# Layer norm in a graph network kernel: group statistics assembled on GpSimd, shifts made on GpSimd

## The chip, the cores and the metric

The kernel runs on one core of one Trainium2 chip. The metric is device time in microseconds, the median over runs. A core has five engines with an instruction queue each, worked off in order: TensorE (PE, matrix products; PEld is its weight loads), VectorE (DVE), ScalarE (ACT), GpSimd (POOL, which also issues the indirect DMAs that gather rows by a list of indices) and SyncE (SP, which issues most other DMAs). An instruction that waits on a semaphore holds up everything behind it in its own queue.

## The reference

A graph of 6250 nodes with 256 channels and 100000 edges. The input is layer-normed over its channels and passed through a ReLU; four rounds of "add the neighbours' rows, three dense layers" follow, and the input is added at the end.

```python
def _layernorm(x, axis=-1, eps=1e-05):
    m = jnp.mean(x, axis=axis, keepdims=True)
    v = jnp.var(x, axis=axis, keepdims=True)
    return (x - m) / jnp.sqrt(v + eps)

h = jnp.maximum(_layernorm(x, axis=-1), 0.0)
x = x + _L0_gnn_ref(h, src, dst, ...)
# in it, for each of 4 layers: h = x + agg(x); three dense layers, ReLU between
```

## The kernel before

The 6250 nodes are 49 blocks of 128 rows, one row to a partition. The kernel first prepares (to about 130 us), then runs the four layers as long chains of matrix products over a count matrix that it builds from the edge lists, with part of the neighbours' rows gathered by GpSimd. Only the preparation is touched by the change; no later instruction moves in any queue.

The preparation interleaves several pieces of work, each written as a generator that gives up control after a short step. The order in which the steps are called is written out by hand, under a manual schedule, so each engine's queue holds its instructions in exactly that order. The pieces that matter here:

- `normed` (the norm). Blocks are loaded in groups of six: group 1 is blocks 0 to 5, group 9 is the last block alone. For a block, VectorE takes statistics of its 256 channels (`bn_stats`, L1007: six numbers, count, mean and a sum of squared distances for the even and for the odd channels) and puts the two halves together (`bn_aggr`, L1008: mean and variance into `mv`). When a group is through, ScalarE takes the square root of its variances (L1015, `std`), and VectorE makes `rstd` by a reciprocal (L1021) and `shift`, minus mean times rstd (L1022). These steps run ahead: the statistics of a pair of blocks are taken six pairs before that pair is scaled.
- For a pair of blocks, ScalarE then scales with ReLU (`h`, L1029), TensorE transposes (L1038), ScalarE copies the result out (`ht`, L1041), TensorE multiplies by the first weight (L1050, into `bp`), VectorE copies that out (`zs`, L1057), ScalarE rounds it (`XY`, high part, L1062), and GpSimd subtracts to get what the rounding left (`XY`, low part, L1067; for four pairs in the middle VectorE does it). SP stores `zs` to a table.
- `look` reads the sorted edge list. VectorE and ScalarE count edges against limits (L768, L771), which gives `starts` (L779). GpSimd then issues 16 indirect gathers (`wd`, L687), four at once and then two between steps of the norm. Four times VectorE unpacks a quarter of them (`hi`, L802, `rel`, L804, `hi`, L806), ScalarE casts (`f`, L807), TensorE transposes (L813) and ScalarE writes the result (`clT`, `cN`, L816, L818).
- `ranking` works on `cN` of all four quarters (L904, L910, L915 to L981). The end of the preparation waits for it and for the last block of the norm.
- `fused` multiplies weight matrices, with a small copy of a bias on GpSimd (L655) for each of three products.

Of the kernel before, what the change touches and what calls it, by code (L numbers as in the profile page):

```python
# [9 lines left out]
F32 = mybir.dt.float32  # L10
# [5 lines left out]
AF = mybir.ActivationFunctionType  # L16
OP = mybir.AluOpType
PSUM = bass.MemoryType.PSUM
DRAM = bass.MemoryType.DRAM
P = 128  # L20
# [400 lines left out]
def sorted_edges(  # L421
# [39 lines left out]
    nc = tc.nc  # L461
    N, C = x.shape
# [84 lines left out]
    eps = const.tile([P, 1], F32, name="eps")  # L547
# [8 lines left out]
    def rows_io(ap, t0, n, sb, load):  # L556

        whole = n if t0 + n < NT or LAST == P else n - 1
        got = []
        if whole:  # L560
            d = ap[t0 * P:(t0 + whole) * P, :].rearrange("(t p) c -> p t c", p=P)
            s = sb[:, :whole, :]
            got.append(nc.sync.dma_start(out=s if load else d, in_=d if load else s))
        if whole < n:
            for r0, r1 in ((0, LAST // 16 * 16), (LAST // 16 * 16, LAST)):
                d = ap[(t0 + whole) * P + r0:(t0 + whole) * P + r1, :]
                s = sb[r0:r1, whole, :]
                got.append(nc.sync.dma_start(out=s if load else d, in_=d if load else s))
        return got
# [31 lines left out]
    def load_w(name, ap, pool, queue, **kw):  # L601
        k = ap.shape[0] // P
        w = pool.tile([P, k, ap.shape[1]], F32, name=name, **kw)
        queue.dma_start(out=w, in_=ap.rearrange("(k p) n -> p k n", p=P))
        return w
# [66 lines left out]
    def after(ins, reason, what=None):  # L672

        what = paced if what is None else what
        if what:
            tc.add_manual_dep(
                ins.ins, what[0],
                mybir.DependencyInfo(mybir.DependencyClass.Sync,
                                     mybir.DependencyReason.DATA),
                reason=reason,  # L680
            )
# [303 lines left out]
    def normed(pool, ps_t, ps_z):  # L985
        G = 6
        w1 = load_w("w1_0", W1s[0], pool, nc.scalar, bufs=1)
        mv = pool.tile([P, NT, nc.vector.BN_AGGR_DIM], F32, name="mv", bufs=1)
        rstd = pool.tile([P, NT], F32, name="rstd", bufs=1)
        shift = pool.tile([P, NT], F32, name="shift", bufs=1)  # L990
        xs, h, ht, zp, zs, stds = {}, {}, {}, {}, {}, []
        pairs = [(i, min(2, NT - i)) for i in range(0, NT, 2)]

        def load(t0):
            n = min(G, NT - t0)
            xs[t0] = pool.tile([P, G, C], F32, name="xs", bufs=4)
            if t0 + n == NT and LAST < P:
                nc.gpsimd.memset(xs[t0][:, n - 1, :], 0.0)
            for got in rows_io(x, t0, n, xs[t0], True):
                if t0 == 2 * G:  # L1000
                    after(got, "the near edges come first", landed)

        def moments(s):
            i0, n = pairs[s]
            for i in range(i0, i0 + n):
                stats = pool.tile([P, nc.vector.BN_STATS_DIM], F32, name="stats", bufs=4)
                nc.vector.bn_stats(stats, xs[i // G * G][:, i % G, :])  # L1007
                got = nc.vector.bn_aggr(mv[:, i, :], stats)  # L1008
            if s == 2:
                landed[:] = [got.ins.name]  # L1010
            if (i0 + n) % G == 0 or i0 + n == NT:
                t0 = (i0 + n - 1) // G * G
                std = pool.tile([P, G], F32, name="std", bufs=2)
                m = i0 + n - t0
                nc.scalar.activation(std[:, :m], mv[:, t0:t0 + m, 1], AF.Sqrt, bias=eps)  # L1015
                stds.append((s, t0, m, std))

        def settle(s):
            while stds and stds[0][0] <= s:
                _, t0, m, std = stds.pop(0)  # L1020
                nc.vector.reciprocal(rstd[:, t0:t0 + m], std[:, :m])  # L1021
                nc.vector.scalar_tensor_tensor(shift[:, t0:t0 + m], mv[:, t0:t0 + m, 0], -1.0,  # L1022
                                               rstd[:, t0:t0 + m], op0=OP.mult, op1=OP.mult)

        def scale(s):
            i0, n = pairs[s]
            h[s] = pool.tile([P, 2, C], F32, name="h", bufs=2)
            for i in range(i0, i0 + n):
                nc.scalar.activation(h[s][:, i - i0, :], xs[i // G * G][:, i % G, :], AF.Relu,  # L1029
                                     bias=shift[:, i:i + 1], scale=rstd[:, i:i + 1])  # L1030

        def turn(s):
            n = pairs[s][1]
            hs = h.pop(s)
            pt = ps_t.tile([P, W], F32, name="agg")
            for c in range(KC):
                for i in range(n):
                    nc.tensor.transpose(pt[:, (c * 2 + i) * P:(c * 2 + i + 1) * P],  # L1038
                                        hs[:, i, c * P:(c + 1) * P], ident)
            ht[s] = pool.tile([P, KC, 2 * P], F32, name="ht", bufs=2)  # L1040
            nc.scalar.copy(ht[s][:, :, :n * P],  # L1041
                           pt.rearrange("p (c n) -> p c n", c=KC)[:, :, :n * P])

        def times(s):
            n = pairs[s][1]
            t = ht.pop(s)
            zp[s] = ps_z.tile([P, W], F32, name="bp")
            for i in range(n):
                for c in range(KC):
                    mm = nc.tensor.matmul(zp[s][:, i * C:(i + 1) * C], t[:, c, i * P:(i + 1) * P],  # L1050
                                          w1[:, c, :], start=(c == 0), stop=(c == KC - 1))
            paced[:] = [mm.ins.name]

        def out(s):
            n = pairs[s][1]
            zs[s] = pool.tile([P, 2, C], F32, name="zs", bufs=5)
            nc.vector.tensor_copy(zs[s][:, :n, :],  # L1057
                                  zp.pop(s)[:, :n * C].rearrange("p (i c) -> p i c", c=C))

        def high(s):  # L1060
            i0, n = pairs[s]
            nc.scalar.copy(XY[:, i0:i0 + n, :C], zs[s][:, :n, :])  # L1062

        def low(s):
            i0, n = pairs[s]
            engine = nc.vector if EASY[0] <= s < EASY[1] else nc.gpsimd
            engine.tensor_tensor(XY[:, i0:i0 + n, C:], zs[s][:, :n, :],  # L1067
                                    XY[:, i0:i0 + n, :C].bitcast(F32), OP.subtract)

        def keep(s):  # L1070
            i0, n = pairs[s]
            rows_io(tables[0], i0, n, zs.pop(s), False)

        for t0 in range(0, 2 * G, G):
            load(t0)
        yield
        for s in range(G):
            moments(s)
        settle(G)
        yield  # L1080
        for t0 in range(2 * G, 4 * G, G):
            load(t0)
        yield
        for s in range(len(pairs) + 5):
            if s % (G // 2) == 0 and s and s * 2 + 3 * G < NT:
                load(s * 2 + 3 * G)
            for lag, f in ((3, out), (4, high), (0, scale), (1, turn), (2, times), (-G, moments),
                           (4, low), (5, keep)):
                if 0 <= s - lag < len(pairs) and (f is not moments or s - lag >= G):
                    f(s - lag)  # L1090
                if f is turn:
                    yield
            settle(s + G - 1)
            yield
# [6 lines left out]
    with tc.manual_schedule():  # L1101
        with tc.tile_pool(name="prep", bufs=2) as prep, tc.tile_pool(
            name="ps_t", bufs=2, space=PSUM
# [3 lines left out]
            ranked = ranking(prep)  # L1107
            next(looked)
            rows = normed(prep, ps_t, ps_z)
            next(rows)  # L1110
            make_identity(nc, ident)
# [866 lines left out]
        with tc.tile_pool(name="hots", bufs=1) as hots, tc.tile_pool(  # L1978
            name="ats", bufs=1
        ) as ats, tc.tile_pool(name="rings", bufs=AHEAD + 2) as rings, tc.tile_pool(  # L1980
            name="gath", bufs=9
        ) as gath, tc.tile_pool(name="nd", bufs=1) as nd, tc.tile_pool(
            name="ps_a", bufs=2, space=PSUM
# [96 lines left out]
```

## Time and profile before

| what | value |
|---|---|
| median of 3 runs | 2004.05 us (2003.39 to 2004.16) |
| profiled execution, its own time | 1999.98 us |
| its span, first to last instruction | 1998.2 us, granted TensorE clock 0.976 on average |
| busy: PE, DVE, ACT, POOL | 1883.4, 1030.9, 1075.0, 1309.6 us |
| the preparation | the first 130 us or so |

Times in the profile count from the start of the span. "Idle before" names what ended an engine's wait. A view by stretches of time gives each engine's busy time in a stretch and the granted TensorE clock as a share of full speed; the timeline lists an engine's instructions with start and length; the chain of waits follows the work that ended last back to what released it at each step.

### The profile page before, as it was taken

The numbers are of one execution on the slowest core, as the hardware profiler recorded it, in microseconds if no ns is written. First come the engines' busy times: TensorE is split into PE (matmuls) and PEld (weight loads), VectorE is DVE, ScalarE is ACT, GpSimd is POOL, SyncE is SP. The second block draws the span as 40 slices with busy tenths as digits, with TensorE's granted clock in tenths as the row PEclk, the third lists the DMA queues.
The fourth block names the chain that finished last, engine by engine and source line by source line (L and its number), as shares of the span: only waits on it lengthen the run. The fifth ranks groups of instructions, "written<-read, shape, count | busy, mean of one in ns | idle before, by whom it ended". The sixth has DMA issues, their size and how long they took to land.

```text
span 1998.2 us, 29053 instructions
## 1 busy us (share of the span) xinstructions
PE 1883.4 (94%) x9236; PEld 1471.0 (74%) x9236; DVE 1030.9 (52%) x2211; ACT 1075.0 (54%) x2166; POOL 1309.6 (66%) x1447
## 2 busy tenths in 40 slices
PE   5856999999999899999999999999999999999997
PEld 3744777777777777777789777777788777777765
DVE  7887887676756343333335443433345354343433
ACT  4745776676767564444445464444445564454442
POOL 2526766766666556777777476676777366777775
PEclk9876999999999999999999999999999999999998
DMA  5524656666656575565557575564657476665653
GB/s 167 177 75 141 202 182 191 199 199 200 208 171 215 160 233 162 173 183 168 181 179 210 160 247 175 154 194 146 196 165 236 147 217 200 186 197 175 181 175 109
DMA packets 252334, 361.40 MB, mean 181 GB/s; under 512 B 33353, under 2 KB 206313, under 8 KB 252155
## 3 DMA queue, kind: packets, MB, share of 16 engines
q1 hardware_dynamic: 188160, 190.34, 30.2%
q0 software_dynamic: 61952, 166.87, 28.0%
q10 hardware_dynamic: 2058, 2.25, 0.4%
q8 instruction: 74, 1.21, 0.2%
q14 instruction: 90, 0.73, 0.1%
HBM read 292.33 MB, written 67.40 MB: 180 GB/s over the span
## 4 chain that ended last, share of the span: by engine, by line
PE 82%; DVE 7%; DMA 5%; issue 3%; POOL 2%; ACT 1%; SPq 0%; DVEq 0%; ACTq 0%; POOLq 0%
PE agg L1942 64%; PE ps L1519 6%; PE ps L1422 6%; DMA rows<-table,idxN 3%; PE bp L1259 2%; PE bp L1050 1%; DVE ws L768 1%; DVE hi L1205 1%; POOL rows L1627 1%; PE pt L1690 1%; POOL lane L1748 1%; DVE lo L1205 1%; PE ps L1436 1%; PE ps L1482 0%; ACT a L1913 0%
## 5 line engine op out<-in xcount | busy, mean ns | idle before, releaser
L1942 PE MATMUL agg<-a,XY 128*128 128x512 f32 (+1 forms) x6272 | 1508.8, 392 | 16.0 <-DVE a L1915 7.3
L1627 POOL DMA_INDIRECT rows<-table,idxN x1121 | 1084.5, 967 | 474.6 <-PE agg L1942 202.6
L1942 PEld LDWEIGHTS agg<-a,XY 128*128 128x128 f32 x6272 | 1142.6, 189 | 249.5 <-issue 12.4
L1913 ACT CAST a<-at 128x512 fp32r<-128x512 uint8 (+1 forms) x1249 | 707.3, 601 | 235.0 <-PE agg L1942 225.7
L1663 DVE TENSOR_TENSOR sums<-sums,rows 128x512 f32<-128x512 f32 x477 | 331.7, 695 | 502.2 <-DMA rows<-table,idxN 461.3
L1915 DVE CAST a<-at 128x512 fp32r<-128x512 uint8 (+1 forms) x312 | 142.0, 460 | 166.3 <-PE agg L1942 143.3
L1267 ACT CAST at<-bp 128x392 uint16<-128x392 f32 x227 | 110.0, 488 | 127.2 <-PE bp L1259 122.0
L1422 PE MATMUL ps<-h,w 128*128 128x512 f32 (+2 forms) x336 | 135.0, 545 | 0.3 <-DVE zz L1524 0.3
L1519 PE MATMUL ps<-w,h 128*128 128x256 f32 x588 | 133.9, 379 | 0.0
L1205 DVE TENSOR_TENSOR lo<-lanes,pairs 128x512 bf16<-128x512 bf16 x256 | 106.7, 422 | 45.6 <-PE bp L1259 44.9
L1259 PEld LDWEIGHTS <-lo 128*128 128x128 bf16 x1028 | 57.0, 102 | 97.3 <-DVE lo L1205 41.4
L1259 PE MATMUL bp<-hi,lo 128*128 128x98 bf16 x1028 | 94.4, 218 | 34.5 <-DVE lo L1205 27.7
L1519 PEld LDWEIGHTS ps<-w,h 128*128 128x128 f32 x588 | 111.5, 190 | 16.0
L596 POOL DMA_INDIRECT table<-zz,ids x72 | 72.5, 1007 | 68.3 <-DVE zz L1524 49.3
L1659 ACT COPY sums<-rows 128x512 f32<-128x512 f32 x74 | 43.8, 592 | 126.4 <-DMA rows<-table,idxN 91.2
L1425 ACT ACTIVATE h<-ps,bias 128x512 f32<-128x512 f32 (+2 forms) x84 | 51.6, 636 | 96.2 <-PE ps L1422 96.1
L1422 PEld LDWEIGHTS ps<-h,w 128*128 128x128 f32 x336 | 62.9, 192 | 52.8 <-issue 37.6
L1698 ACT ACTIVATE h<-pt,bias 128x256 f32<-128x256 f32 (+1 forms) x84 | 33.0, 444 | 127.7 <-PE pt L1690 127.7
L1524 DVE TENSOR_TENSOR zz<-ps,w 128x512 f32<-128x512 f32 (+1 forms) x81 | 50.5, 638 | 96.6 <-PE ps L1519 83.2
L1349 DVE TENSOR_TENSOR XY<-back,XY 128x256 fp32r<-128x256 f32 x138 | 54.7, 422 | 46.3 <-ACT XY L1348 45.9
L1956 ACT ACTIVATE h<-agg,bias 128x512 f32<-128x512 f32 (+1 forms) x60 | 37.3, 669 | 72.5 <-PE agg L1942 72.3
L1205 DVE TENSOR_TENSOR hi<-hi,pairs 128x784 bf16<-128x784 bf16 x128 | 72.7, 568 | 4.4
(239 smaller groups left out, 957.3 us busy)
## 6 DMA issues: line engine op xcount, KB each, us to landing
at<-mat SPq DMA_DIRECT2D x140, 448.0 KB
mat<-at SPq DMA_DIRECT2D x32, 784.0 KB
at<-mat SPq DMA_DIRECT2D x62, 336.0 KB
rows<-table,idxN POOLq DMA_INDIRECT x1121
back<-table SPq DMA_DIRECT2D x138, 128.0 KB
table<-zz SPq DMA_DIRECT2D x35, 256.0 KB
at<-mat SPq DMA_DIRECT2D x63, 112.0 KB
own<-zz SPq DMA_DIRECT2D x55, 128.0 KB
```

Of the source, the lines that this page charges most:

```text
L596: got = nc.gpsimd.indirect_dma_start(out=ap, out_offset=bass.IndirectOffsetOnAxis(ap=ids[:, b:b + 1], axis=0), in_=sb, in_offset=None)
L1205: nc.vector.tensor_tensor(o, values, which[:, :, None, :].to_broadcast(shape), op)
L1259: mm = nc.tensor.matmul(bp[:, m * HW:(m + 1) * HW], lo[:, m, :], hi[:, m, :], start=(i == 0), stop=(i == len(sets) - 1))
L1267: nc.scalar.copy(o, v)
L1349: later(1, lambda: nc.vector.tensor_tensor(XY[:, j:j + m, C:], z[:, :m, :], XY[:, j:j + m, :C].bitcast(F32), OP.subtract))
L1422: mm = nc.tensor.matmul(ps[:, :w], weights[l][0][:, c, i * P:(i + 1) * P], h1[:, c, :w], start=(c == 0), stop=(c == KC - 1))
L1519: mm = nc.tensor.matmul(o, h2[0][:, c, nodes], w3[:, c, :], start=(c == 0), stop=(c == KC - 1))
L1627: got = nc.gpsimd.indirect_dma_start(out=t[:, c % 2, :], out_offset=None, in_=tables[self.l][:, :], in_offset=bass.IndirectOffsetOnAxis(ap ...
L1663: nc.vector.tensor_tensor(sums, sums, rows.rearrange("p h c -> p (h c)"), OP.add)
L1913: nc.scalar.copy(o, v)
L1915: nc.vector.tensor_copy(o, v)
L1942: mm = nc.tensor.matmul(agg[c][:, :w], XY[:, j, o:o + P], a[:, :w], start=(i == 0 and half == 0), stop=(i == NT - 1 and half == 1))
```

## The change

From group 3 on, `bn_aggr` is gone. The six raw statistics of each block stay in one tile for the whole group, and when the group is through, GpSimd puts mean and variance together for up to six blocks at once in seven small instructions of 128 x 6: difference of the two means, sum of the means, sum of the squared distances, the difference scaled, squared, added to the sum, and the mean scaled by -0.5 (so `mv` then holds minus the mean). The square root on ScalarE carries the division by 256 in its scale. The shift becomes one product on GpSimd instead of VectorE. Groups 1 and 2 stay as they were.

```diff
         def moments(s):
             i0, n = pairs[s]
+            plain = i0 < 2 * G
             for i in range(i0, i0 + n):
-                stats = pool.tile([P, nc.vector.BN_STATS_DIM], F32, name="stats", bufs=4)
-                nc.vector.bn_stats(stats, xs[i // G * G][:, i % G, :])
-                got = nc.vector.bn_aggr(mv[:, i, :], stats)
+                if i % G == 0:
+                    parts[0] = pool.tile([P, G, nc.vector.BN_STATS_DIM], F32, name="stats", bufs=2)
+                stats = parts[0]
+                got = nc.vector.bn_stats(stats[:, i % G, :], xs[i // G * G][:, i % G, :])
+                if plain:
+                    got = nc.vector.bn_aggr(mv[:, i, :], stats[:, i % G, :])
...
-                nc.scalar.activation(std[:, :m], mv[:, t0:t0 + m, 1], AF.Sqrt, bias=eps)
+                mean, var = mv[:, t0:t0 + m, 0], mv[:, t0:t0 + m, 1]
+                if not plain:
+                    even, odd = (stats[:, :m, 3 * k:3 * k + 3] for k in range(2))
+                    apart = pool.tile([P, G], F32, name="apart", bufs=2)[:, :m]
+                    nc.gpsimd.tensor_tensor(apart, even[:, :, 1], odd[:, :, 1], OP.subtract)
+                    nc.gpsimd.tensor_tensor(mean, even[:, :, 1], odd[:, :, 1], OP.add)
+                    nc.gpsimd.tensor_tensor(var, even[:, :, 2], odd[:, :, 2], OP.add)
+                    nc.gpsimd.tensor_scalar(apart, apart, math.sqrt(C) / 2, None, op0=OP.mult)
+                    nc.gpsimd.tensor_tensor(apart, apart, apart, OP.mult)
+                    nc.gpsimd.tensor_tensor(var, var, apart, OP.add)
+                    nc.gpsimd.tensor_scalar(mean, mean, -0.5, None, op0=OP.mult)
+                nc.scalar.activation(std[:, :m], var, AF.Sqrt, bias=eps,
+                                     scale=1.0 if plain else 1.0 / C)
...
                 nc.vector.reciprocal(rstd[:, t0:t0 + m], std[:, :m])
-                nc.vector.scalar_tensor_tensor(shift[:, t0:t0 + m], mv[:, t0:t0 + m, 0], -1.0,
-                                               rstd[:, t0:t0 + m], op0=OP.mult, op1=OP.mult)
+                if t0 < 2 * G:
+                    nc.vector.scalar_tensor_tensor(shift[:, t0:t0 + m], mv[:, t0:t0 + m, 0], -1.0,
+                                                   rstd[:, t0:t0 + m], op0=OP.mult, op1=OP.mult)
+                else:
+                    nc.gpsimd.tensor_tensor(shift[:, t0:t0 + m], mv[:, t0:t0 + m, 0],
+                                            rstd[:, t0:t0 + m], OP.mult)
```

Where the instructions stand is seen in the queues. First GpSimd's, in the stretch of the gathers (L687), around the end of group 5; the low parts are L1067 before and L1087 after, since the code behind the edit moved by 20 lines. Before:

```order
L1067 TENSOR_TENSOR XY<-zs,XY 128x2x256
L687 DMA wd<-joined,starts 98x128 x2
L1067 TENSOR_TENSOR XY<-zs,XY 128x2x256
L687 DMA wd<-joined,starts 98x128 x2
L1067 TENSOR_TENSOR XY<-zs,XY 128x2x256
```

And now:

```order
L687 DMA wd<-joined,starts 98x128 x2
L1023 TENSOR_TENSOR apart<-stats 128x6
L1024 TENSOR_TENSOR mv<-stats 128x6
L1025 TENSOR_TENSOR mv<-stats 128x6
L1026 TENSOR_SCALAR apart<-apart 128x6
L1027 TENSOR_TENSOR apart<-apart 128x6
L1028 TENSOR_TENSOR mv<-mv,apart 128x6
L1029 TENSOR_SCALAR mv<-mv 128x6
L1087 TENSOR_TENSOR XY<-zs,XY 128x2x256
L687 DMA wd<-joined,starts 98x128 x2
L1087 TENSOR_TENSOR XY<-zs,XY 128x2x256
L1042 TENSOR_TENSOR shift<-mv,rstd 128x6
```

The seven stand behind gathers 7 and 8 and ahead of the low part and gathers 9 and 10; the shift of the group stands ahead of gathers 11 and 12. The seven of group 6 stand between gathers 14 and 15 in the same way, the shift of group 4 between gathers 4 and 5.

Second, ScalarE's queue at the same place, with what each instruction waits for (a semaphore of the named engine). Before:

```order
L1041 COPY ht<-agg 128x512 [waits PE_49,Activation_49]
L1015 ACTIVATE std<-mv,eps 128x6 [waits DVE_49]
L807 CAST f<-hi 98x512 [waits DVE_49]
L1062 CAST XY<-zs 128x2x256
L1029 ACTIVATE h<-xs,shift,rstd 128x256 [waits DMAHW3_49,Activation_49]
```

And now:

```order
L1061 COPY ht<-agg 128x512 [waits PE_49,Activation_49]
L1030 ACTIVATE std<-mv,eps 128x6 [waits Pool_49]
L807 CAST f<-hi 98x512 [waits DVE_49]
L1082 CAST XY<-zs 128x2x256
L1049 ACTIVATE h<-xs,shift,rstd 128x256 [waits DMAHW3_49,Activation_49]
```

The order is the same; the square root waits for GpSimd (for L1028, the sixth of the seven) where it waited for VectorE.

Third, VectorE's queue at the start of group 6, where the reciprocal of group 5 stands. Before:

```order
L1057 COPY zs<-bp 128x512
L1007 BN_STATS stats<-xs 128x6
L1008 BN_AGGR mv<-stats 128x2
L1007 BN_STATS stats<-xs 128x6
L1008 BN_AGGR mv<-stats 128x2
L1021 RECIPROCAL rstd<-std 128x6
L1022 SCALAR_TENSOR_TENSOR shift<-mv,rstd 128x6
```

And now:

```order
L806 TENSOR_SCALAR hi<-wd 98x512
L1077 COPY zs<-bp 128x512
L1010 BN_STATS stats<-xs 128x6 x2
L1037 RECIPROCAL rstd<-std 128x6
L1077 COPY zs<-bp 128x512
```

Two `bn_aggr` of a pair and the shift are gone; the reciprocal stays at its place.

More of the change, by code (lines that the diff above doesn't have):

```diff
@@ L990, in normed @@
         shift = pool.tile([P, NT], F32, name="shift", bufs=1)
-        xs, h, ht, zp, zs, stds = {}, {}, {}, {}, {}, []
+        xs, h, ht, zp, zs, stds, parts = {}, {}, {}, {}, {}, [], [None]
         pairs = [(i, min(2, NT - i)) for i in range(0, NT, 2)]
```

## The prediction

> **What bounds the kernel now.** I read the page first. The chain of work that ended last is mostly TensorE in the layers, which this change doesn't touch; what counts is how long the preparation takes, since everything behind it waits for its last store. So I went to the busy time by stretches, then to GpSimd's and ScalarE's timelines between 52 and 84 us. The stretches (length, then busy time with counts of PE, PEld, DVE, ACT and POOL, then granted clock, DMA share, GB/s):
>
> ```profile
> 26.00:52.00 26.00, 21.47 (x100) 17.22 (x100) 25.35 (x55) 20.93 (x44) 3.39 (x4) 1.00 0.38 120
> 52.00:58.50 6.50, 6.50 (x38) 5.73 (x37) 4.69 (x17) 6.39 (x14) 5.28 (x5) 1.00 0.93 269
> 58.50:64.00 5.50, 2.72 (x17) 1.98 (x14) 3.22 (x4) 0.15 (x2) 4.65 (x6) 1.00 0.83 259
> 64.00:80.00 16.00, 14.67 (x68) 11.57 (x68) 15.32 (x36) 11.82 (x28) 12.93 (x12) 0.79 0.48 148
> ```
>
> Up to 52 us VectorE is full (25.35 of 26.0) and GpSimd nearly idle (3.39). From 52 us it turns round. GpSimd's timeline (start, length, instruction, idle time before it):
>
> ```profile
> 52.15 1.08 POOL L687 DMA_INDIRECT wd<-joined,starts  x1 [1.08 <-DVE zs L1057]
> ...
> 56.09 0.97 POOL L687 DMA_INDIRECT wd<-joined,starts  x1 [0.30 <-issue]
> 57.09 1.29 POOL L1067 TENSOR_TENSOR XY<-zs,XY 128x512 fp32r<-128x512 f32 x1
> ...
> 63.84 0.96 POOL L687 DMA_INDIRECT wd<-joined,starts  x1 [0.30 <-issue]
> 64.83 1.28 POOL L1067 TENSOR_TENSOR XY<-zs,XY 128x512 fp32r<-128x512 f32 x1
> ...
> 75.56 0.97 POOL L687 DMA_INDIRECT wd<-joined,starts  x1 [0.30 <-issue]
> 76.83 0.97 POOL L687 DMA_INDIRECT wd<-joined,starts  x1 [0.30 <-PE agg L1038]
> 78.11 0.97 POOL L687 DMA_INDIRECT wd<-joined,starts  x1 [0.31 <-issue]
> ```
>
> These are gathers 1, 4, 8, 14, 15 and 16. From 52.15 to 79.08 the queue has no gap over the 0.3 us that each gather takes to issue. The low part at 64.83 shows the backlog, beside ScalarE's timeline:
>
> ```profile
> 56.03 0.63 ACT L1062 CAST XY<-zs 128x512 fp32r<-128x512 f32 x1
> ...
> 58.23 0.30 ACT L1015 ACTIVATE std<-mv,eps 128x6 f32<-128x6 f32 x1
> 63.88 0.62 ACT L807 CAST f<-hi 98x512 f32<-98x512 int32 x1 [5.35 <-DVE hi L806]
> ...
> 73.46 0.30 ACT L1015 ACTIVATE std<-mv,eps 128x6 f32<-128x6 f32 x1
> ...
> 74.30 0.64 ACT L1062 CAST XY<-zs 128x512 fp32r<-128x512 f32 x1
> ...
> 85.71 0.62 ACT L807 CAST f<-hi 98x512 f32<-98x512 int32 x1 [1.51 <-DVE hi L806]
> ```
>
> Its high part was ready at 56.66 (56.03 + 0.63), so it stood 8.2 us in GpSimd's queue. Here GpSimd is a full server in order, and whatever is put into it is late by the backlog and makes all behind it later. The chain of waits ends on it too, with gather 16:
>
> ```profile
> 78.11 5.80 DMA wd<-joined,starts
> ```
>
> VectorE's unpacking of the last quarter then starts at 83.94 (row below), 0.68 us idle before it, and the ranking and the end of the preparation follow. The rows at 58.23 and 73.46 are the square roots of groups 5 and 6, taken as soon as ScalarE comes to them.
>
> **The change part by part.** Taken off VectorE: 37 `bn_aggr` and 7 shifts. Rows of VectorE, with the group of all 37:
>
> ```profile
> 57.04 0.42 DVE L1007 BATCH_NORM_STATS2 stats<-xs 128x6 f32<-128x256 f32 x1
> 57.49 0.18 DVE L1008 BATCH_NORM_AGGREGATE mv<-stats 128x2 f32<-128x6 f32 x1
> 57.59 0.40 DVE L1007 BATCH_NORM_STATS2 stats<-xs 128x6 f32<-128x256 f32 x1
> ...
> 76.00 0.66 DVE L1067 TENSOR_TENSOR XY<-zs,XY 128x512 fp32r<-128x512 f32 x1
> ...
> 83.94 0.43 DVE L802 TENSOR_SCALAR hi<-wd 98x512 int32<-98x512 int32 x1 [0.68 <-DMA wd<-joined,starts]
> ```
>
> ```profile
> L1008 DVE BATCH_NORM_AGGREGATE mv<-stats 128x2 f32<-128x6 f32 x37 | 6.7, 182 | 1.3
> ```
>
> A block now takes 0.55 us of VectorE (57.04 to 57.59). Without `bn_aggr` the next statistics need not wait for the one before; bounds are 0.42 us (nothing overlaps) and, at the overlap of the row at 57.59 with the aggregate ahead of it (57.49 + 0.18 - 57.59 = 0.08), 0.34. I take 0.34, since both are VectorE instructions with nothing to wait for: 0.21 saved a block, 37 x 0.21 = 7.8 us of VectorE in all, and about 0.2 for each shift. On the path that counts for little. In the full stretch six pairs and a shift give 6 x 0.42 + 0.2 = 2.7 us, but gather 1 also waits for a matrix product (L1050) and a low part that hang on ScalarE, and ScalarE is delayed there: the square root of group 3 waits 1.9 us (below) for GpSimd where it waited 0.2, less some 1.0 by which the statistics end earlier, about 0.5 us late. I count gather 1 at its old time; bounds 0.35 earlier and 0.4 later.
>
> Put on GpSimd, a group: seven instructions of 128 x 6 and a shift. No such instruction is in the trace; the nearest rows are, grouped by form and from the timeline:
>
> ```profile
> L841 POOL TENSOR_TENSOR size<-less 98x16 f32<-98x16 f32 x1 | 0.3, 323 | 0.0
> ...
> L718 POOL TENSOR_SCALAR edge<-edge 128x17 f32<-128x17 f32 x1 | 0.3, 301 | 0.1
> ```
>
> ```profile
> 17.19 0.26 POOL L877 CAST what<-place 128x24 bf16<-128x24 f32 x1
> 17.34 0.25 POOL L878 CAST what<-colf 128x24 bf16<-128x24 f32 x1
> ```
>
> Upper bound: five products and sums at 0.32, two at 0.30, and 0.1 for each of three waits within the seven (the 0.1 idle before L718, which waits for its own engine): 5 x 0.32 + 2 x 0.30 + 0.3 = 2.5 us. Lower bound: start to start 0.15 (17.19 to 17.34) for all seven, 1.05. Three of the seven do wait for the one before and four don't, so I take 4 x 0.15 + 3 x 0.42 = 1.9, say 2.0 for the seven, 1.9 until the square root can start (six of them and the signal), and 0.3 for a shift (bounds 0.15 and 0.4).
>
> One rule speaks for the lower bound: the Trainium skill (Perfetto Trace Analysis, GPSIMD Engine Instruction) says that a GpSimd span is unreliable and that start-to-start spacing is to be used. By it the seven cost 1.05 and the shift 0.15, and the result below would be 2.2 us lower; the spacing row is of instructions that don't wait for each other, which three of the seven do.
>
> Now the place. Group 5: the seven stand behind gather 8, which ends at 64.80 (63.84 + 0.96) plus the 0.3 of the shift of group 4 in front: the square root starts at 65.1 + 1.9 = 67.0 and not at 58.23. Of this ScalarE's own idle time until 63.88 covers 5.35; its cast L807, queued behind the root, starts 3.4 us late, and the high parts and scalings with it. VectorE's reciprocal of the group waits too. This stall is overtaken by the next. Group 6: ahead of the end of gather 14 (75.56 + 0.97 = 76.53) GpSimd has done one shift, seven, and one shift more: 76.53 + 0.3 + 2.0 + 0.3 = 79.1, and the root of group 6 starts at 79.1 + 1.9 = 81.0, not 73.46: 7.5 us late, since GpSimd's queue, not ScalarE, sets it. Bounds by the two prices: 76.53 + 0.15 + 1.05 + 0.15 + 0.9 = 78.8 (5.3 late) and 76.53 + 0.4 + 2.5 + 0.4 + 2.4 = 82.2 (8.8 late). Gathers 15 and 16 come 2.6 + 2.0 = 4.6 us later, which alone would put the last quarter 4.6 later; so ScalarE's lateness is the longer path: root, the high part at 74.30, VectorE's low part at 76.00, then the third quarter.
>
> Regained: the high part ended at 74.94 and VectorE came to it only at 76.00; it has then long done what held it, so 1.06 comes back: 7.5 - 1.1 = 6.4. Behind that, groups 7 and 8 find GpSimd less full; a root there waits 1.9 instead of 0.2 behind statistics that end 0.4 earlier, 1.3 us, which I take as covered by ScalarE's later wait for TensorE; bounds 0 and 1.3. VectorE's savings there (0.4 a pair) I count at nothing, since TensorE's L910 stands behind a scaling on ScalarE; bound 0.9 gained.
>
> **Sum**: 6.4 us on the profiled execution, 1999.98 + 6.4 = 2006.4. The median shown is 2004.05, 4.07 above that execution, so the prediction for it is 2004.05 + 6.4 = 2010.4.
>
> **Rivals.** First, collisions make it worse. In the view of one line, VectorE's L804 takes:
>
> ```profile
> L804 DVE TENSOR_TENSOR rel<-hi,node x4: 691/694/2034, 62.7 to 84.5; 98x512 f32<-98x512 int32 x4
> ```
>
> Three times 0.69 us and once 2.03, the one time that it ran beside a GpSimd low part. The added instructions read the same memory and can hold such a one, or be held by it; and in the stretch of 64 to 80 us, behind TensorE's idle time, the granted clock is 0.79, so a longer stall makes TensorE slow again. One long collision (1.3) and one slow start (the matrix products lose about 2) on top of 6.4, with the upper price (8.8 - 7.5 = 1.3), give 11.0: 2015.0. Against it: L804 of the second quarter may just as well miss the low part that held it. The Trainium skill (SBUF — State Buffer, Who interferes with whom) says that a VectorE instruction with two inputs in SBUF and a GpSimd one that reads it shut each other out for a whole instruction; the trace agrees (2.03 against 0.69).
>
> Second, the stall is absorbed. ScalarE idles elsewhere (1.5 us before the last cast L807 at 85.71 alone), and what follows the root of group 6 may hang less on it than I think: then only gather 16 counts, at the lower price 0.15 + 1.05 + 0.15 + 1.05 = 2.4 us late, less the 0.68 of waiting that is already there in other work: about +2, 2006.
>
> Third, the other side: VectorE is the bound and the relief shows. It decides if GpSimd gets to the seven before ScalarE gets to the root, at groups 5 and 6 above all; then 2.7 us up to gather 1 and 0.9 ahead of the ranking come off, 3.6 in all, 2000.4. For it speaks the stretch 26 to 52 us, VectorE at 25.35 of 26.0; against it the queue order, with the seven behind gathers 8 and 14 in a queue that has no gap.
>
> **How the numbers follow.** A measurement here tells about 0.2% (4.0 us) from no change. The late queue 0.61, collisions 0.14, absorbed 0.15, relief 0.10, half of that beyond 4.0 us. Slower: 0.61 + 0.14 = 0.75; same: 0.15 + 0.05 = 0.20; faster 0.05. The forecast's own range is +3.9 (5.3 - 1.1 - 0.35 for an earlier gather 1, rounded) to +9.4 (8.8 - 1.1 + 0.4 + 1.3), 2008 to 2013.5. The range that should hold 8 in 10 takes in half of the absorbed case and most of the collisions: 2006.3 to 2014.5.
>
> **What would show it.** Right: the root of group 6 starts near 81 us and GpSimd's L1028 ends just before it; ScalarE shows a wait of some 3 us ahead of the root of group 5 beyond its old idle time and some 5 at group 6; gather 16 ends near 83.7; the last unpacking L802 comes near 90; the first build instruction of VectorE (130.20 before) comes some 6 us later, and all behind it by the same. Wrong: the roots start before 59 and 75 us; or GpSimd's seven take under 1 us; or the preparation ends late and the layers take it back.

## The result, and the profile after

| | before | changed |
|---|---|---|
| median of 12 runs each | 2001.71 us (1998.63 to 2004.31) | 2008.04 us (2004.33 to 2010.28) |
| profiled execution, its span, granted clock | 1999.98 us, 1998.2 us, 0.976 | 2010.28 us, 2008.4 us, 0.971 |
| preparation: first L768 to the first build instruction | 106.41 us | 110.67 us |

The ratio of the runs is 1.0024, with a 95% interval of 1.0016 to 1.0033: the change makes the kernel slower by some 4.8 us (3.2 to 6.6). The medians of the table are 6.3 us apart, which lies inside that interval. The prediction was 2010.4 us and slower.

The profiled executions differ by 10.3 us, so a trace of the whole program can't be read against the other trace by its end. The third row of the table can be. It is the time from VectorE's first count to its first build instruction, within one execution. VectorE's rows, before:

```profile
23.79 1.62 DVE L768 TENSOR_SCALAR_CACHE_REDUCE ws<-near 98x1408 bf16<-98x1408 f32 x1
...
76.97 0.43 DVE L802 TENSOR_SCALAR hi<-wd 98x512 int32<-98x512 int32 x1
...
130.20 0.57 DVE L1205 TENSOR_TENSOR hi<-cols,pairs 128x784 bf16<-128x784 bf16 x1 [2.86 <-ACT pairs L1193]
```

and in the changed kernel:

```profile
24.91 1.62 DVE L768 TENSOR_SCALAR_CACHE_REDUCE ws<-near 98x1408 bf16<-98x1408 f32 x1
...
81.85 0.69 DVE L1087 TENSOR_TENSOR XY<-zs,XY 128x512 fp32r<-128x512 f32 x1 [3.84 <-ACT XY L1082]
...
82.56 0.38 DVE L802 TENSOR_SCALAR hi<-wd 98x512 int32<-98x512 int32 x1
...
84.72 0.74 DVE L1010 BATCH_NORM_STATS2 stats<-xs 128x6 f32<-128x256 f32 x2
...
89.30 0.42 DVE L802 TENSOR_SCALAR hi<-wd 98x512 int32<-98x512 int32 x1
...
135.58 0.57 DVE L1225 TENSOR_TENSOR hi<-cols,pairs 128x784 bf16<-128x784 bf16 x1 [2.85 <-ACT pairs L1213]
```

The changed execution is already 1.12 us late at its first L768, in code that both kernels share; from there to the build it takes 110.67 instead of 106.41 us, 4.26 more, which agrees with the ratio. The rest of the 10.3 us lies in front of L768 and, some 4.9 of it, in the layers, where it was not followed. All times below are therefore also given from the first L768, "after L768".

The view by stretches, over the same four as before (length, then busy time and counts of PE, PEld, DVE, ACT and POOL, clock, DMA share, GB/s):

```profile
26.00:52.00 26.00, 21.52 (x95) 17.50 (x96) 22.86 (x42) 21.16 (x46) 5.78 (x19) 1.00 0.34 109
52.00:58.50 6.50, 6.50 (x39) 5.80 (x38) 4.14 (x10) 6.50 (x16) 5.36 (x6) 1.00 0.99 294
58.50:64.00 5.50, 3.34 (x19) 2.47 (x17) 3.59 (x5) 0.37 (x1) 4.83 (x7) 1.00 0.89 258
64.00:80.00 16.00, 10.69 (x48) 8.42 (x48) 7.84 (x17) 7.93 (x18) 13.68 (x24) 0.79 0.44 128
```

In the first row VectorE went from 25.35 to 22.86 us of work, and nothing came of it: gather 1 starts 27.86 us after L768, 28.36 before (28.66 in a second execution of the changed kernel). In the last stretch GpSimd has 0.75 us more to do, and all others fall off: VectorE from 15.32 to 7.84, ScalarE from 11.82 to 7.93, TensorE from 14.67 to 10.69. They wait. GpSimd's timeline shows for what:

```profile
64.64 0.97 POOL L687 DMA_INDIRECT wd<-joined,starts  x1 [0.30 <-issue]
65.64 0.21 POOL L1023 TENSOR_TENSOR apart<-stats 128x6 f32<-128x6 f32 x1
...
66.84 0.20 POOL L1028 TENSOR_TENSOR mv<-mv,apart 128x6 f32<-128x6 f32 x1
67.00 0.23 POOL L1029 TENSOR_SCALAR mv<-mv 128x6 f32<-128x6 f32 x1
67.21 1.28 POOL L1087 TENSOR_TENSOR XY<-zs,XY 128x512 fp32r<-128x512 f32 x1
...
77.92 0.97 POOL L687 DMA_INDIRECT wd<-joined,starts  x1 [0.31 <-issue]
78.91 0.22 POOL L1023 TENSOR_TENSOR apart<-stats 128x6 f32<-128x6 f32 x1
...
82.20 1.18 POOL L687 DMA_INDIRECT wd<-joined,starts  x1 [0.30 <-issue]
```

The seven of group 5 start when gather 8 ends, those of group 6 when gather 14 ends. They take 67.21 - 65.64 = 1.57 us. The last row is gather 16. ScalarE's queue, with the square roots of groups 5 and 6 (its roots):

```profile
67.07 0.30 ACT L1030 ACTIVATE std<-mv,eps 128x6 f32<-128x6 f32 x1 [8.20 <-POOL mv L1028]
...
80.34 0.30 ACT L1030 ACTIVATE std<-mv,eps 128x6 f32<-128x6 f32 x1 [5.35 <-POOL mv L1028]
...
81.18 0.64 ACT L1082 CAST XY<-zs 128x512 fp32r<-128x512 f32 x1
```

ScalarE stands still for 8.2 and 5.35 us behind a 0.3 us instruction whose result no scaling needs for three pairs of blocks. Of the 8.2 us some 5.35 were idle in the kernel before too (ahead of its L807 at 63.88); the 5.35 us at group 6 are new, since the root at 73.46 had waited for nothing. VectorE's reciprocal of group 5, which stands one pair behind the root, waits 2.69 us for it (at 67.40). The chain of waits, which in this stretch had run through TensorE and gather 16 before, now runs through GpSimd's queue:

```profile
77.92 0.97 POOL wd L687
78.91 0.22 POOL apart L1023
...
80.11 0.21 POOL mv L1028
80.55 0.31 ACT clT L816
...
81.30 0.52 ACT XY L1082
81.82 0.99 ACT h L1049 x2
82.86 0.55 PE agg L1058 x3
83.40 3.29 PE bp L1070 x8
```

It goes gather 14, seven, root, then what is queued behind the root: the copies, the high part, the scaling, the transposes.

### The profile page after: what moved, and what is told of

It is laid out like the page before. It is cut to its first block, busy times and chain, and to the rows that moved or that the text cites. A ratio compares the mean times of both kernels' runs of the same rounds, so it can differ in the third digit from the quotient of the medians.

```text
span 2008.4 us, 29070 instructions
## 1 busy us (share of the span) xinstructions
PE 1887.4 (94%) x9236; PEld 1474.9 (73%) x9236; DVE 1018.5 (51%) x2167; ACT 1075.4 (54%) x2166; POOL 1323.2 (66%) x1503
## 3 DMA queue, kind: packets, MB, share of 16 engines
HBM read 292.33 MB, written 67.40 MB: 179 GB/s over the span
## 4 chain that ended last, share of the span: by engine, by line
PE 83%; DVE 5%; DMA 4%; POOL 3%; issue 3%; ACT 2%; SPq 0%; ACTq 0%; DVEq 0%; POOLq 0%
PE agg L1962 65%; PE ps L1539 6%; PE ps L1442 6%; DMA rows<-table,idxN 2%; PE bp L1279 2%; PE bp L1070 1%; POOL rows L1647 1%; POOL lane L1768 1%; DVE hi L1225 1%; PE pt L1710 1%; DVE lo L1225 1%; PE ps L1456 1%; PE ps L1502 0%; POOL wd L687 0%; DVE sums L1683 0%
```

## Experiments

Some of these ran on chips that granted a lower clock (0.94 to 0.95, where the kernel before took 2177.5 and 2200.2 us, against 0.972 to 0.978 and 2003.1 us on another), and the ratios' intervals are as wide as the effect or nearly so. A run without a ratio in the table is one execution, whose whole time tells nothing: after_again took 2198.3 us beside the 2200.2 of the kernel before. The preparation's length, read in each trace, is finer. I split it at the start of the last L802, the unpacking of the last quarter of the gathers: up to there the queues of the norm and of the gathers set the time, behind it come the ranking and the last pairs.

| kernel | L768 to last L802, us | against 60.2 | last L802 to build, us | whole, us | ratio to before |
|---|---|---|---|---|---|
| before, before_again | 60.15, 60.26 | | 46.26, 45.79 | 106.41, 106.05 | |
| changed, after_again | 64.39, 65.71 | +4.2, +5.5 | 46.28, 44.74 | 110.67, 110.45 | 1.0024 (1.0016 to 1.0033) |
| only_5_6 | 64.74 | +4.5 | 46.38 | 111.12 | 1.0017 (1.0001 to 1.0033) |
| only_5 | 61.94 | +1.7 | 46.01 | 107.95 | |
| only_6 | 63.75 | +3.5 | 45.09 | 108.84 | |
| only_7_8_9 | 60.16 | 0.0 | 44.81 | 104.97 | 1.0013 (0.9996 to 1.003) |
| without_5_6 | 60.05 | -0.2 | 44.76 | 104.81 | 0.9999 (0.999 to 1.0009) |
| seven_on_vector | 59.69 | -0.5 | 46.31 | 106.00 | 1.0009 (0.9993 to 1.0024) |
| gathers_late_alone | 60.88 | +0.7 | 46.67 | 107.55 | |
| root_6_late_alone | 65.65 | +5.4 | 46.69 | 112.34 | |
| root_two_pairs_later | 64.96 | +4.8 | 46.52 | 111.48 | 1.0024 (1.0009 to 1.004) |
| root_later_shift_on_vector | 59.63 | -0.6 | 48.30 | 107.93 | |

The expectations give the whole; the first part is what tells the theories apart. The second part moves by up to 2 us, also between two executions of one kernel: 46.28 and 44.74 us for the changed one. The view of that stretch (one row of the first execution, then one of after_again) shows the granted clock behind it, 0.85 and 0.89:

```profile
89.30:135.60 46.30, 36.91 (x275) 29.59 (x273) 30.80 (x69) 26.98 (x61) 24.89 (x38) 0.85 0.26 85
```

```profile
90.10:134.90 44.80, 35.39 (x276) 28.61 (x274) 30.86 (x69) 27.02 (x61) 24.90 (x38) 0.89 0.27 88
```

TensorE has 1.5 us more to do in the one for the same products, all of the difference. The clock isn't all that moves this part: root_6_late_alone took 46.69 us in it at 0.92, with 35.03 us of TensorE work. So differences of that size in the second part are not read.

### The same two kernels once more

> The kernel before once more, to see how far the length of the preparation repeats from one execution to another, and on this chip: 106.4 us again, within 0.5, if it is set by the queues; more than 1 us away, and differences of that size between the other runs say nothing.

> The changed kernel once more, for the spread of the length of the preparation: 110.7 us again within 0.5 (the kernel before had 106.4 and 106.05).

Both within 0.4 us in the whole, though in after_again by 1.3 us more ahead of the last L802 and 1.5 less behind it. The change costs 4.3 us in the whole (110.56 against 106.23 by the means) and 4.85 up to the last L802 (65.05 against 60.2), beside 4.8 by the ratio. The late roots repeat: ScalarE's waits are 8.17 and 5.08 us in after_again.

### Which groups cost

One condition says which groups (counted from 0 in the code) stay on VectorE; the condition for the shift is the same on `t0`. For only_5_6:

```diff
-            plain = i0 < 2 * G
+            plain = i0 // G not in (4, 5)
```

and in the same place `i0 < 6 * G` for only_7_8_9, `i0 // G in (0, 1, 4, 5)` for without_5_6, `!= 4` and `!= 5` for only_5 and only_6.

> Groups 5 and 6 alone are put together on GpSimd (seven instructions and the shift); groups 3, 4, 7, 8 and 9 stay as in the kernel before. The measure within one trace is the length of the preparation from the first count L768 on VectorE to VectorE's first build instruction: 106.4 us in the kernel before, 110.7 in the changed one. Late queue: these two groups carry the cost, since they stand behind gathers 8 and 14: preparation 110 to 111 us, ratio 1.002 to 1.0025; the root of group 5 waits some 8 us and that of group 6 some 5 for GpSimd. Rival, the amount of work on GpSimd costs wherever it stands: two of some six groups' worth, preparation about 108, ratio 1.0008. Rival, VectorE's relief in the other groups pays part of the cost back in the changed kernel: then it is missing here, preparation 111.5 or more.

> Groups 7, 8 and 9 alone are put together on GpSimd; groups 3 to 6 stay as in the kernel before. Late queue: GpSimd has no backlog there, so next to no cost: preparation 106 to 107 us (106.4 before, 110.7 in the changed kernel), ratio 1.000, gather 16 at its old place. Rival, the amount of work: two and a sixth of six groups' worth, about 108, ratio 1.0008. Rival, collisions with VectorE at the shared memory: the instructions L1026 and L1027 of group 7, which took 0.95 and 0.72 us in the changed kernel, do so again or hold VectorE, and the preparation is 1 to 2 us longer.

> Groups 3, 4, 7, 8 and 9 are put together on GpSimd, groups 5 and 6 on VectorE as before: the changed kernel without the two that stand among the gathers. Late queue: no root waits there, VectorE is relieved in the stretch up to 52 us and behind the gathers. With 105.0 us for groups 7 to 9 alone and up to 2.7 us of relief ahead of gather 1, the preparation takes 103.5 to 105.5 us (106.4 before, 110.7 in the changed kernel), ratio 0.9985 to 0.9995. Rival, the relief brings nothing: 106.4. Rival, small work on GpSimd costs wherever it stands: 109.

> Group 5 alone is put together on GpSimd, all other groups as in the kernel before. By the steps of the prediction the root of group 5 starts near 66.5 us and ScalarE stops for 3 us beyond its old idle time; behind it ScalarE had 1.8 us of idle time ahead of the second cast L807 and 2.4 ahead of the third, which take up part of it, and gathers 9 to 16 come 1.8 us later: preparation 107 to 108 us (106.4 and 106.05 before, 111.1 for groups 5 and 6 together). Rival, the first stop already carries the cost: 109 or more.

> Group 6 alone is put together on GpSimd, at its place of the changed kernel (between gathers 14 and 15), all other groups as in the kernel before. With no other seven in front, the root of group 6 starts 1.4 us behind the end of gather 14, at 78.0 in the times of the kernel before instead of 73.5: 4.5 later, less 1.06 that VectorE had waited for other work: preparation 109.5 to 110 us. With group 5 it is 6.1 later by the same sum and was measured at 111.1. Rival, it is the first stop that counts: 107 or less.

Groups 5 and 6 alone cost what the whole change costs, 4.5 us up to the last L802 against 4.85, with roots that wait 8.17 and 5.29 us; the whole, 111.12, is just above what was expected. In without_5_6 nothing is lost there (-0.2), though the seven of groups 3 and 4 run on GpSimd ahead of the gathers: the amount of work on GpSimd is not what costs, only its place. Nor does VectorE's relief gain anything up to the last L802. Of groups 7 to 9 this part says little: in only_7_8_9 the seven of group 7 start 57.97 us after L768, 2.2 ahead of the last L802, and those of groups 8 and 9 come behind it. For them there is the whole, 104.97 and 104.81 us, below the 106 to 107 expected of only_7_8_9 and no longer than before. Both kernels are short behind the last L802 (44.8 us), which would be a gain of 1.2 us. But after_again (44.74) and only_6 (45.09), one with and one without the groups 7 to 9 on GpSimd, are as short, so whether the change in these groups shortens that part stays open. In only_7_8_9 the root of group 8, with the ranking's L915 queued behind it, waits for GpSimd:

```profile
95.32 0.30 ACT L1030 ACTIVATE std<-mv,eps 128x6 f32<-128x6 f32 x1 [1.15 <-POOL mv L1028]
```

no longer than it waited for VectorE's aggregates in the kernel before:

```profile
94.97 0.30 ACT L1015 ACTIVATE std<-mv,eps 128x6 f32<-128x6 f32 x1 [2.03 <-DVE mv L1008]
```

only_5 came out at +1.7, as expected in the whole; only_6 at +3.5 up to the last L802, which is the expected 4.5 less 1.06, while its whole is 0.7 below the expectation for the short second part. In it the root waits 6.71 us for GpSimd and comes 54.09 us after L768, 4.2 later than the mean of before (49.67 and 50.04). The two alone make +5.2, both together +4.5, a difference within the 1.3 us by which two executions of the changed kernel differ there.

without_5_6 has the shortest preparation of all, but its time is not told from the kernel before (0.9999, 0.999 to 1.0009). No version was found that is faster than the kernel before.

### The same arithmetic on VectorE

```diff
-                    nc.gpsimd.tensor_tensor(apart, even[:, :, 1], odd[:, :, 1], OP.subtract)
+                    nc.vector.tensor_tensor(apart, even[:, :, 1], odd[:, :, 1], OP.subtract)
...
-                    nc.gpsimd.tensor_tensor(shift[:, t0:t0 + m], mv[:, t0:t0 + m, 0],
+                    nc.vector.tensor_tensor(shift[:, t0:t0 + m], mv[:, t0:t0 + m, 0],
```

> The combined form is kept from group 3 on, but the seven instructions and the shift are VectorE's; GpSimd's queue is that of the kernel before. Late queue: no cost; VectorE gives up some 6 x 0.2 us a group and takes seven small ones at some 0.1 to 0.15, so the preparation is 106 to 106.5 us (106.4 before, 110.7 in the changed kernel), ratio 0.9995 to 1.0. Rival, the new form itself costs (one tile of statistics for a whole group with two buffers, or the longer chain from the last statistics to the root): preparation 108 or more. Rival, the engine is nothing and the amount of small work everything: VectorE is the fuller engine up to 52 us, and the preparation is longer than 107.5.

Both parts are those of the kernel before. The new form itself costs nothing; the engine and its queue do. VectorE's first and last of the seven of group 6:

```profile
70.20 0.17 DVE L1023 TENSOR_TENSOR apart<-stats 128x6 f32<-128x6 f32 x1
...
70.94 0.35 DVE L1029 TENSOR_SCALAR mv<-mv 128x6 f32<-128x6 f32 x1
71.01 0.68 DVE L1087 TENSOR_TENSOR XY<-zs,XY 128x512 fp32r<-128x512 f32 x1
```

The seven take 0.81 us from the first to the next instruction, half of GpSimd's 1.57.

### Late gathers or a late root

The seven do two things: they delay the gathers behind them, and the root waits for them. Two kernels do one each. The first keeps the aggregates and lets GpSimd do the seven of groups 5 and 6 into tiles that nobody reads:

```diff
-            plain = i0 < 2 * G
+            plain = True
...
-                if not plain:
+                if t0 // G in (4, 5):
...
-                    nc.gpsimd.tensor_tensor(var, var, apart, OP.add)
+                    nc.gpsimd.tensor_tensor(over, over, apart, OP.add)
```

> The kernel before (aggregates and shifts on VectorE everywhere), and beside it the seven instructions of groups 5 and 6 on GpSimd at their places of the changed kernel, writing tiles that nobody reads: no root waits for GpSimd, only the gathers behind the seven come later, by 1.6 us after group 5 and 3.2 after group 6. If the delay of the gathers is enough to move the end: gather 16 at 57.5 us after the first L768 (54.3 before), last L802 at 63.3 (60.15), preparation 109.0 to 109.7 us (106.4 before). If only ScalarE's stop at the root counts: not above 107.

The second has the seven and the root of group 6 alone, emitted at the start of the next step, behind the gathers:

```diff
             if s % (G // 2) == 0 and s and s * 2 + 3 * G < NT:
                 load(s * 2 + 3 * G)
+            together()
```

> Group 6 alone is put together on GpSimd, its seven instructions behind gathers 15 and 16 and its root on ScalarE right behind them, ahead of the high part as before; all other groups as in the kernel before. No gather is delayed, but the root waits until 1.4 us after the end of gather 16, 80.5 instead of 73.5 in the times of the kernel before, 7.0 later. If the late root carries the cost, as the prediction has it: the third L802 some 6 us later, preparation 112 us, 7.0 less 1.06 above the 106.4 of before. If the gathers carry it: not above 107.

The late root alone costs 5.4 us up to the last L802 and 6.1 in the whole, with no gather delayed (gather 16 at 54.18 us after L768; 54.32 before). ScalarE's root in it, and VectorE's third unpacking:

```profile
80.84 0.30 ACT L1038 ACTIVATE std<-mv,eps 128x6 f32<-128x6 f32 x1 [6.59 <-POOL mv L1036]
```

```profile
82.39 0.39 DVE L802 TENSOR_SCALAR hi<-wd 98x512 int32<-98x512 int32 x1
```

The root is 56.66 us after L768, 6.8 later than before, and the third L802 58.21, 4.9 later than the 53.18 and 53.55 of before. The expectation of 112 us held, with 0.7 us of it from the part behind the last L802; the third L802 had been expected some 6 us later.

The late gathers alone cost 0.7 us up to the last L802, far less than the 3.15 by which this L802 would come later if the gathers set the end. Gather 16 starts 58.04 us after L768, 3.5 later than in the two executions of before, and yet the last quarter is unpacked only 0.7 later. GpSimd's and VectorE's rows:

```profile
82.50 1.31 POOL L687 DMA_INDIRECT wd<-joined,starts  x1 [0.30 <-DMA table<-zs]
```

```profile
85.34 0.43 DVE L802 TENSOR_SCALAR hi<-wd 98x512 int32<-98x512 int32 x1
```

From the gather's start to the instruction that reads it pass 2.84 us, where gather 16 took 5.80 before. The delay was made up in the transfer (what shortened it was not tried). What the late gathers do hold up is a quarter earlier: the third L802 waits 2.28 us for its gathers and comes 54.57 us after L768, 1.2 later than before.

```profile
79.03 0.43 DVE L802 TENSOR_SCALAR hi<-wd 98x512 int32<-98x512 int32 x1 [2.28 <-DMA wd<-joined,starts]
```

The whole, 107.55, falls between the two numbers expected, and 0.7 of its 1.3 us lie behind the last L802, in the part that varies.

### Taking ScalarE's wait away

Both kernels emit the roots, and what hangs on them, two pairs later; the seven stay.

```diff
+                due = s if plain else s + 2
+                roots.append((due, std[:, :m], var, 1.0 if plain else 1.0 / C))
...
+                if f is moments:
+                    root(s + G)
```

> As the changed kernel, but the square roots on ScalarE, and the reciprocals and shifts that hang on them, stand two pairs of blocks later in their queues from group 3 on, so that ScalarE need not stop for GpSimd. The seven stay where they are, so gathers 9 to 16 are as late as in the changed kernel. It splits the cost: if ScalarE's stop at the root carries all of it, the preparation goes back to 106.5 to 107.5 us (106.4 before, 110.7 in the changed kernel), ratio 1.000; if the delay of the last gathers is the longer path, it stays at 110 to 110.7, ratio 1.002. I expect two paths of nearly the same length: gather 16 is issued at 82.20 in the changed kernel and may land some 5.5 us later, at 87.7, so the last L802 (89.30 there) comes at about 88, and the preparation takes 109 to 109.7, ratio 1.0015.

That missed: +4.8 up to the last L802, nothing gained. No root waits any more, and the third L802 is 3.6 us earlier than the changed kernel's mean (54.45 after L768 against 57.65 and 58.41). But now scalings stop ScalarE, one for 4.22 us at 69.12 and this one:

```profile
82.29 1.09 ACT L1054 ACTIVATE h<-xs,shift,rstd 128x256 f32<-128x256 f32 x2 [4.32 <-POOL shift L1047]
```

The shift of group 5, pushed back with its root, stood behind gather 14 and the seven of group 6 on GpSimd. The wait had only changed its place. With the shift on VectorE as well:

> As root_two_pairs_later, but with the shift on VectorE, so that no scaling waits for GpSimd's queue; the seven stay on GpSimd at their places. There the stop had moved from the root to the scaling, which waited 4.3 us for the shift L1047 behind the seven of group 6. If it is ScalarE's waiting for GpSimd that costs, wherever it sits, nothing is left but the late gathers (107.55 alone) less what VectorE is relieved (1.4 in the run with groups 7 to 9): preparation 106 to 107.5 us. If the place of the seven in GpSimd's queue costs by itself: 109 or more.

```profile
77.15 0.50 DVE L802 TENSOR_SCALAR hi<-wd 98x512 int32<-98x512 int32 x1 [2.33 <-DMA wd<-joined,starts]
...
84.11 0.66 DVE L802 TENSOR_SCALAR hi<-wd 98x512 int32<-98x512 int32 x1
```

The last L802 is 59.63 us after L768, 0.6 earlier than in the kernel before, with the seven still on GpSimd, gather 16 still late (56.65) and no wait of ScalarE for GpSimd up to there. Part of that is a gain at another place, since gather 1 starts 26.65 us after L768, 1.7 earlier than before:

```profile
51.13 1.09 POOL L687 DMA_INDIRECT wd<-joined,starts  x1 [0.21 <-PE ps L789]
```

Even with all of the 1.7 given back the cost would be 1.1 us, against 4.85 in the changed kernel. So most of the cost up to there was ScalarE's wait. The whole preparation is 0.4 us above what I expected: the second part takes 48.30 us, the longest of all, at the lowest granted clock of all, 0.82, with TensorE busy for 38.78 us. The roots of groups 8 and 9 come later in it as well, and what each of the two costs was not followed.

## Why the prediction was right, and where its sizes were off

**The mechanism.** The late queue is shown: the seven start at the ends of gathers 8 and 14, the roots wait, the same arithmetic on VectorE costs nothing, the same work of groups 3 and 4 on GpSimd, ahead of the gathers, costs nothing up to the last L802, and a late root alone costs what the steps give (6.8 later, less 1.06, makes 5.7; +5.4 up to the last L802, +6.1 in the whole). The root of group 6 starts 55.4 and 56.2 us after L768 where 49.7 and 50.0 were before: 6.0 later, predicted 7.5. The marks named for it came: ScalarE's waits, some 3 us beyond the old idle time at group 5 (8.20 - 5.35 = 2.85) and some 5 at group 6 (5.35), the root near 81 (80.34), L1028 just ahead of it, gather 16 ending near 83.7 (83.38), the last L802 near 90 (89.30), all in an execution that began 1.1 us late.

**The price of the seven.** I took 2.0 us for the seven, 1.9 until the square root can start, and 0.3 for a shift; they take 1.57, 1.43 (65.64 to 67.07) and 0.2. With these the sum reads 76.53 + 0.2 + 1.57 + 0.2 + 1.43 = 79.9, 6.5 late instead of 7.5. The root came 6.0 late, since gather 14 was only 1.4 us later (53.01 and 53.77 us after L768, against 51.77 and 52.14) and not the 2.0 of one seven and two shifts. The nearest rows were of wider tiles (16 and 17 columns at 0.30 to 0.32 us); at 6 columns an instruction takes 0.2. The rule that start-to-start spacing is to be used (the Trainium skill, Perfetto Trace Analysis, GPSIMD Engine Instruction) would have made it 1.05 with the spacing of the row at hand, whose instructions don't wait for each other. The trace agrees where an instruction waits for nothing (65.64, 65.80 and 65.96, 0.16 apart) and not for those that wait for the one before, which stand some 0.3 apart.

**What is regained.** The 1.06 us of VectorE ahead of its low part came back as worked out: the low part at 81.85, one of the five pairs (not four) for which VectorE makes it, starts as ScalarE's high part ends (81.18 + 0.64), and the third L802 is 4.3 and 5.0 us late.

**The sum.** With the measured prices 6.5 - 1.06 = 5.4; measured 4.85 up to the last L802 (4.2 and 5.5) and 4.8 (3.2 to 6.6) by the ratio; predicted 6.4. The whole times alone wouldn't rule out 6.4; it is the traces that show less. The mis-sized term is the price of the seven and the shifts, 1.0 us of the 1.6. The rest, 0.5 to 0.6 us, is within what two executions differ by. VectorE's savings, counted at nothing, brought nothing that can be told, and gather 1 kept its time (27.86 and 28.66 us after L768; 28.36 and 28.39 before). The later roots of groups 7 and 8, counted as covered, show no cost that stands out of the 2 us by which the second part moves: it is not longer than before.

**Its place in the time shown.** The forecast of 2010.4 was 6.4 above a median of 2004.05 of three runs; over 12 runs that median is 2001.71. So nearly all of the 2.4 us by which 2008.04 lies below the forecast is the starting point, 2.3 too high. That the medians then lie 6.3 apart, as good as the 6.4, is luck in part: the traces show 4.3 us in the whole preparation and 4.85 up to the last L802.

**"... = 4.6 us later, which alone would put the last quarter 4.6 later", of gathers 15 and 16.** Wrong, though it didn't enter the sum: 3.5 us later put the last L802 only 0.7 later. I took the 5.80 us of gather 16 for a fixed time.

**"This stall is overtaken by the next."** It is, where both are there: the root of group 6 waits 5.35 us for GpSimd (5.29 in only_5_6), so by then ScalarE is no longer late by the first stall. What group 5 adds is GpSimd's queue ahead of that root, which comes 55.89 us after L768 in only_5_6 and 54.09 in only_6. Alone, group 5 costs 1.7 us.

**The rivals.** Collisions didn't lengthen it. The view of the lines that read the gathers, in the changed kernel (shortest, median, longest in ns):

```profile
L804 DVE TENSOR_TENSOR rel<-hi,node x4: 691/693/694, 60.8 to 89.8; 98x512 f32<-98x512 int32 x4
```

```profile
L806 DVE TENSOR_SCALAR hi<-wd x4: 426/440/1925, 61.5 to 90.6; 98x512 int32<-98x512 int32 x4
```

L804 has lost its 2 us, and one L806, 0.43 in all quarters before, has taken them over; the first L802, 1.95 before, takes 0.43. (Which of them is hit changes between executions: in before_again two L804 took 2.19 and 2.03.) A slow start of TensorE stands in the chain above (eight products in 3.29 us at 83.40), but from the third to the last L802 pass 6.74 and 7.30 us, 6.97 and 6.71 before, so it adds nothing that can be told. Absorbed is out, since the late root's delay goes through to the build. Of the relief nothing is seen in the full stretch that spoke for it: 2.5 us of VectorE's work went there, and gather 1 hardly moved. In root_later_shift_on_vector it did come 1.7 us earlier, with the roots later as well; which of the two brought that was not separated.

## What to carry to other kernels

Before work is moved to the less busy engine, look at the place in its queue where it lands, and at who waits there: GpSimd was idle for most of the 26 us ahead of its gathers (3.39 us of work) and full for the 27 us of them, and only the two groups whose seven landed among the gathers cost anything that can be told. The price is paid by the engine that waits in order: a 0.3 us root that no scaling needed yet held ScalarE for 8.2 and 5.35 us (of the first, 5.35 were idle before as well), so a waiting instruction is worth moving down its queue, but with all that hangs on it, or the wait turns up at another place. Where an effect is as small as the spread between executions, measure a stretch within one trace, between two instructions that both kernels have, end it ahead of the part that the clock moves, and take it twice.

## What had not been expected of the hardware

Small GpSimd instructions are stretched beside VectorE's low part. GpSimd's timeline of the changed kernel, group 7:

```profile
88.52 0.20 POOL L1025 TENSOR_TENSOR mv<-stats 128x6 f32<-128x6 f32 x1
88.81 0.95 POOL L1026 TENSOR_SCALAR apart<-apart 128x6 f32<-128x6 f32 x1
89.85 0.72 POOL L1027 TENSOR_TENSOR apart<-apart 128x6 f32<-128x6 f32 x1
```

L1026 took 0.24 and L1027 0.19 us in group 5. Here they run beside VectorE's low part (88.69, 0.69 us) and its L804 (89.83, 0.69 us). Together they are 1.24 us longer, and ScalarE's root of the group waits 0.95 us. In after_again the two took 1.02 and 0.72 us.

VectorE's five comparisons L904 are the other side of that. By groups of instructions, before and in the changed kernel:

```profile
L904 DVE TENSOR_SCALAR wd<-cN 128x768 bf16<-128x768 bf16 x5 | 3.5, 757 | 0.0
```

```profile
L904 DVE TENSOR_SCALAR wd<-cN 128x768 bf16<-128x768 bf16 x5 | 1.4, 350 | 0.0
```

Before, a low part of GpSimd (89.58 to 90.86) and most of a second (91.55 to 93.04) ran beside them; in the changed kernel GpSimd was idle from 93.57 to 95.11, over the first half of them (94.36 to 95.78), and the low part that it began at 95.11 took 1.81 us instead of 1.28. Over the 14 executions of all kernels it goes by what meets: 3.44 to 3.56 us in the seven where two low parts ran beside the five, 2.49 to 2.53 in the five where one did, 1.42 in the two of the changed kernel. It is no gain at the end: in the changed kernel TensorE's L910, which reads what they write, starts 71.65 us after L768, 7.26 behind the last L802, and before 67.35, 7.20 behind it.
